# Layer 3 of a GNN stack: the keys split into two equal halves, and a tile's logits issued in two runs

## The chip, the cores and the metric

The kernel runs on one core of a Trainium2 chip. A core has a tensor engine (TensorE, PE in the profile, with its weight loads listed apart as PEld), VectorE (DVE), ScalarE (ACT), GpSimd (POOL) and SyncE (SP), each with an instruction queue of its own that is served in order, and DMA queues that move data between device memory and the on-chip memory. Matmuls write to PSUM, which has eight banks of 512 f32 values on each of 128 partitions. The metric is the device time of one execution, in microseconds (us).

## The reference

Four graph layers over 3327 nodes with 256 features, each a residual block `x = x + layer(relu(layernorm(x)))`. The change touches the last one, which runs two steps of attention with nucleus (top-p) sparsification beside a propagation by the row-normalized adjacency:

```python
def _top_p_attention(X, W1, W2, W3):
    q = X @ W1.T @ W2.T
    k = X @ W3.T
    logits = q @ k.T / TAU
    probs = jax.nn.softmax(logits, axis=-1)
    ...
    keep_sorted = cs - sp < TOP_P
    ...
    A = probs * mask
    return A / jnp.maximum(A.sum(-1, keepdims=True), 1e-12)
...
for n in range(STEPS):
    A = _top_p_attention(Xa, W1, W2, W3)
    Xf = R @ Xf
    Xa = A @ Xa
    Z = Z + Xf @ U1[n].T + Xa @ U2[n].T
h = X + Z
```

The queries and keys have 64 features. All of it is f32. So for each of 128 query rows a full row of 3327 logits is made, exponentiated, cut at the smallest set of entries that holds 0.9 of its sum, and multiplied with the 3327 x 256 values.

## The kernel before

**Tiles.** Nodes stand in T = 26 tiles of P = 128 (3328, one row more than there are nodes); H = 13 is half of them. Layers 0 to 2 take the first 950 us or so and are not touched, except that their last stage fills the first step's keys.

**Keys and queries.** A key has 64 features and PE 128 rows, so the keys lie in two halves of the partitions: `kT` has the first LOW = 12 tiles of keys on partitions 0 to 63 and the other HIGH = 14 on partitions 64 to 127 (`add_nodes`, L233; `new_keys`, L256). `add_nodes` computes key and query of one tile of nodes with two matmuls (L241), lets ACT copy the key into its half with a running sum for the mean (L249) and the query into qT (L253), and a DMA from ACT's queue copies the query to the other half too (L254). `centre` (L893) takes the mean off the keys on DVE, one instruction for each half.

**A tile's logits.** `logits_steps` (L904) is a generator. In each of the first three turns it makes one pair of PSUM banks from the pool `ps_row` (two buffers of two banks): one matmul of the low 64 partitions with 512 keys of the low half (L912), one of the high 64 partitions with 512 keys of the high half, into the two banks. ACT evicts both with one exponential of 1024 columns into the row e, and a sum into one column of `parts` (L935). The fourth turn makes the 255 keys that are left, of the high half alone (L921). POOL clears the last column of e beforehand (L931), in `scores`; the general path (`redone`) does the same at L1171.

**The search.** `search_steps` (L939) finds the threshold of each row. DVE sums `parts` (total, L951); ACT takes its logarithm and from that a first threshold (mean, lnv, c, t at L952 to L956); ACT runs two passes over e (L967, L969); DVE runs two more passes (L977, and L986 in four pieces with 26 MAX8 of 128 columns, L990), five rounds of the largest eight (v, L995 and L998), and at the end one pass that zeroes what is not kept (L1006).

**Attention times values.** `rows_times_steps` (L168) turns e by blocks of 128 on PE (L177, four blocks to a bank of `ps_tr`), ACT copies them out (eT, L180), and PE multiplies them with the values (L188), 26 matmuls of 256 columns. `Rows.begin` turns the first two groups of four blocks ahead of time, `Rows.finish` does the rest.

**Propagation.** `propagated_steps` (L1051) is the other product: 26 matmuls (f, L1062) with a tile's 26 blocks of the adjacency, loaded by SP as two slabs of 13 blocks (L1059, three buffers); POOL adds the identity to the block on the diagonal (L1061). It yields after each block, and a plan, a dictionary from block number to a list of functions, says what PE is given behind which block.

**The order.** PE's instructions are in the order in which they are recorded (`manual_schedule`); the other engines' orders are set by a scheduler. A period of the first step, for tile m: finish the attention of m (with the first two passes of the search of a later tile put behind its first groups), then propagate m + 3 with this plan: the four turns of the logits of tile m + 3 behind blocks 0, 2, 4 and 6 (`spread`, L1295), the attention's result turned behind block 3 (`turn`), its key and query made behind 10 (`node`), its values behind 14 (`values`), and the next tile's first two groups turned behind 22 (`rows.begin`). The second step has the four turns at the same blocks and `rows.begin` behind 22; `finish3` ends with a normalization on DVE and POOL (L1126 to L1138) and stores the output. At the start of either step a few tiles are prepared first: in step 0 tile 0's logits go behind blocks 9, 11, 13 and 15 of the second propagation and tile 1's behind 0, 2, 4 and 6 of the third; in step 1 tile 0's come alone, and tiles 1 and 2 are spread over one propagation each, with `PropagationOfFirstStep.turn` behind block 2 and `sums` (L1115) behind 10. At the end of step 0 (m from 20 on) there is no propagation in the period, and the turns come one behind the other.

Of the kernel before, what the change touches and what calls it, by code (L numbers as in the profile page):

```python
# [11 lines left out]
F32 = mybir.dt.float32  # L12
# [9 lines left out]
N = 3327  # L22
D = 256
DA = 64
P = 128
T = 26
NP = T * P
LAST = N - (T - 1) * P
NC = D // P
H = T // 2  # L30
# [1 line left out]
TOPK = 700  # L32
TOP_P = 0.9
EPS = 1e-5
LOW = 12
HIGH = T - LOW
Z90 = 1.2815516
PDF90 = 0.1754983
# [7 lines left out]
def kernel(  # L46
# [22 lines left out]
    nc = tc.nc  # L69
# [186 lines left out]
    def new_keys(name, pool):  # L256
        kT = pool.tile([P, HIGH * P], F32, tag="kT", name=f"kT_{name}")
        ksum = pool.tile([P, T], F32, tag="ksum", name=f"ksum_{name}")
        nc.gpsimd.memset(ksum, 0.0)
        return kT, ksum  # L260


# [576 lines left out]
    def layer_3_in(tag, big, ep, w3, sm3, h3, kT0, ksum0, left):  # L839
# [59 lines left out]
                    k = kT[r : r + DA, :n]  # L899
                    nc.vector.tensor_scalar(k, k, mean[r : r + DA, :], None, ALU.add)  # L900

        CHUNKS = (NP - 256) // 1024

        def logits_steps(kT, q, e, name, evict):  # L904


            main = e[:, : CHUNKS * 1024].rearrange("p (h c n) -> p h c n", h=2, n=512)
            for c in range(CHUNKS + 1):
                pl = ps_row.tile([P, 2, 512], F32, tag="row", name=f"pl_{name}_{c}")
                if c < CHUNKS:  # L910
                    for h in range(2):
                        nc.tensor.matmul(  # L912
                            pl[:, h, :], q[h * DA : (h + 1) * DA, :],
                            kT[h * DA : (h + 1) * DA, c * 512 : (c + 1) * 512],
                            start=True, stop=True,
                        )
                    evict(c, main[:, :, c, :], pl)
                    yield c
                else:
                    n = N - CHUNKS * 1024  # L920
                    nc.tensor.matmul(  # L921
                        pl[:, 0, :n], q[DA:, :], kT[DA:, c * 512 : c * 512 + n], start=True, stop=True
                    )
                    evict(c, e[:, CHUNKS * 1024 : N], pl[:, 0, :n])
                    yield c

        def scores(step, m, kT):

            name = f"{tag}{step}_{m}"
            e = ep.tile([P, NP], F32, tag="e", name=f"e_{name}")  # L930
            nc.gpsimd.memset(e[:, N:], 0.0)  # L931
            parts = sm3.tile([P, CHUNKS + 1], F32, tag="parts", name=f"parts_{name}")

            def evict(c, dst, src):
                nc.scalar.activation(dst, src, AF.Exp, accum_out=parts[:, c : c + 1])  # L935

            return e, parts, logits_steps(kT, qT[:, m * P : (m + 1) * P], e, name, evict)
# [230 lines left out]

        def redone(step, m, kT, name, evict):
            e = ep.tile([P, NP], F32, tag="e", name=f"e_{name}")  # L1170
            nc.gpsimd.memset(e[:, N:], 0.0)  # L1171
            run(logits_steps(kT, queries(step, m, name), e, name, evict))
            return e

# [91 lines left out]
        with tc.manual_schedule(engines=PE_ALONE):  # L1266

            st0, made, dens, props = new_state("0"), {}, {}, []

            def prepare(step, m, kT):  # L1270
                made[m] = scores(step, m, kT)
                return made[m][2]

            def find(step, m, st):
                return search_steps(step, m, *made[m][:2], st, dens)

            def passes(finder):


                if finder is None:  # L1280
                    return {}
                next(finder)

                def one_more():
                    with tc.issue_after(last_turned[-1].ins):
                        next(finder, None)

                return {0: [one_more], 2: [one_more], 3: [lambda: next(finder, None)]}

            def propagate_first(m, at):  # L1290
                acc = new_acc(f"f0_{m}")
                run(propagated_steps(acc, 0, m, h3), at)
                props.append(PropagationOfFirstStep(m, acc))

            def spread(steps, first=0, gap=2):  # L1295

                return {first + gap * i: [lambda: next(steps, None)] for i in range(CHUNKS + 1)}

            class Rows:


                def __init__(self, step, values):
                    self.step, self.values, self.begun = step, values, {}

                def begin(self, m):
                    if m < T:
                        name = f"a{self.step}_{m}"
                        accs = []

                        def acc():  # L1310
                            accs.append(new_acc(name))
                            return accs[0]

                        steps = rows_times_steps(acc, made.pop(m)[0], self.values, w3, name)
                        next(steps)
                        self.begun[m] = steps, accs

                def finish(self, m, at=None):
                    steps, accs = self.begun.pop(m)
                    run(steps, at)  # L1320
                    return accs[0]

            for i in range(EARLY):
                if i == 0:
                    left.pool = w3, "eT", 3
                    propagate_first(0, dict(zip((14, 20), ([what] for what in left.stages))))
                    mean0 = key_sum(kT0, ksum0, "0")
                elif i == 1:
                    steps = prepare(0, 0, kT0)
                    propagate_first(1, merged({3: [lambda: centre(kT0, mean0(), "0")]}, spread(steps, 9)))  # L1330
                    run(find(0, 0, st0))
                else:
                    first, second = prepare(0, i - 1, kT0), None
                    propagate_first(i, spread(first))
                    finder = find(0, i - 1, st0)
                    run(finder)
            run(prepare(0, EARLY - 1, kT0))
            finder = find(0, EARLY - 1, st0)
            rows = Rows(0, h3)
            rows.begin(0)  # L1340
            for m in range(T):
                plan = passes(finder)
                if props:
                    p = props.pop(0)
                    plan = merged(plan, {1: [p.turn], 5: [p.sums]})
                a = AttentionOfFirstStep(m, rows.finish(m, plan), dens.pop(m), f"{m}")
                after = {3: [a.turn], 10: [a.node], 14: [a.values], 22: [lambda: rows.begin(m + 1)]}
                steps = prepare(0, m + AHEAD, kT0) if m + AHEAD < T else iter(())
                if m + EARLY < T - LATE:
                    propagate_first(m + EARLY, merged(spread(steps), after))  # L1350
                else:
                    run(steps)
                    for k in sorted(after):
                        after[k][0]()
                finder = find(0, m + AHEAD, st0) if m + AHEAD < T else None
            flags0 = failed("0", st0)
            propagate_first(T - LATE, {})
# [11 lines left out]
        with tc.manual_schedule(engines=PE_ALONE):  # L1369
            centre(kT1, key_sum(kT1, ksum1, "1")(), "1")  # L1370
            st1 = new_state("1")
            run(prepare(1, 0, kT1))
            run(find(1, 0, st1))
            for i in range(1, LATE):
                plan = spread(prepare(1, i, kT1))
                p = props.pop(0)
                propagate_first(T - LATE + i, merged(plan, {2: [p.turn], 10: [p.sums]}))
                finder = find(1, i, st1)
                if i + 1 < LATE:
                    run(finder)  # L1380
            p = props.pop(0)
            p.turn()
            p.sums()

            def propagate_second(m, at):
                acc = new_acc(f"f1_{m}")
                run(propagated_steps(acc, 1, m, fs), at)
                return acc

            rows = Rows(1, vs)  # L1390
            rows.begin(0)
            for m in range(T):
                acc = rows.finish(m, passes(finder))
                y = attention_of_second_step(m, acc, dens.pop(m), f"{m}")
                plan = spread(prepare(1, m + AHEAD, kT1)) if m + AHEAD < T else {}
                plan = merged(plan, {22: [lambda: rows.begin(m + 1)]})
                finish3(m, y, propagate_second(m, plan), f"{m}")
                finder = find(1, m + AHEAD, st1) if m + AHEAD < T else None
            flags1 = failed("1", st1)
# [77 lines left out]
```

## Time and profile before

| what | us |
|---|---|
| three runs, median | 2720.22 (2718.76 to 2723.25) |
| the profiled execution | 2722.73 |
| its span, first to last instruction | 2720.9 |
| first propagation of layer 3 begins on PE | 956 |
| step 0 of layer 3, periods with propagation and logits | 1022.85 to 1722.86 |
| its last six tiles and step 1's start | 1722.86 to 1930.63 |
| step 1, periods with logits | 1930.63 to 2627.83 |

The profile's page lists busy time by engine, the span in 40 slices, the DMA queues, the chain that ended last, and the costliest groups of instructions. In a group or a timeline row, `f<-fsa,slab3a 128*128 128x256 f32` is output, inputs, weights (rows x columns) and output (partitions x columns); `x8` counts instructions, and a bracket gives the idle time of the engine ahead of the row and what ended it. The granted TensorE clock, in tenths, and the busy share of PE in the same 40 slices (68 us each):

```profile
PE   7999999999999979999999999987999999999997
...
PEclk9999999999999999999999999998999999999998
```

PE is nearly always busy; the slices with less are the kernel's start and end, the start of layer 3 (slice 15 from the left) and the end of step 0 with the start of step 1 (slices 27 and 28); the clock is lower in slice 28 and at the end. The exponential that evicts a pair of banks, and then the two groups that make a tile's logits, in step 1 and in step 0, from the listing of PE's groups:

```profile
L935 ACT ACTIVATE e_a<-pl_a 128x1024 f32<-128x1024 f32 x208 | 179.4, 863 | 183.4 <-PE pl_a L912 150.4
```

```profile
L912 PE MATMUL pl_a<-kT_1a,qT 64*128 64x512 f32 x312 | 92.0, 665 | 6.6 <-ACT e_a L935 5.0 <-DMA slab3a<-in_adj_t_dram 1.5
L912 PE MATMUL pl_a<-kT_0a,qT 64*128 64x512 f32 x312 | 87.0, 638 | 2.3 <-ACT e_a L935 2.3
L921 PE MATMUL pl_a<-kT_1a,qT 64*128 64x255 f32 x52 | 18.5, 437 | 0.0
L921 PE MATMUL pl_a<-kT_0a,qT 64*128 64x255 f32 x52 | 18.1, 427 | 0.0
```

Behind the bar stand the busy time of the group in us, the mean of one in ns, and the idle time of the engine just ahead of it with what ended it. The durations of matmuls that run side by side or overlap in the pipeline add up to more than they take; what they cost is better read from the starts of the rows behind them in a timeline.

### The profile page before, as it was taken

Reading aid. Unit: us, or ns where it says so; the run is one execution under the profiler, and the core shown is the slowest. Engines: PE = TensorE matmul, PEld = TensorE weight load, DVE = VectorE, ACT = ScalarE, POOL = GpSimd, SP = SyncE. Lnnn points to the kernel's source line nnn. Section 1 sums busy time; section 2 is a strip of 40 time slices with the busy share of each in tenths; the row PEclk is TensorE's granted clock in tenths of the full one; section 3 lists DMA queues with packets and bytes.
Section 4 is the critical chain, followed back from the end, with each engine's and each line's share of the span. In section 5 each row is a group of like instructions: output and inputs, shape, how many; then the busy total and the mean of one; then the engine's idle time right before and its main releaser. Section 6 shows DMA issues by size and latency. Waiting matters only on the chain. (4 is left out here: it accounts for less than half of the span.)

```text
span 2720.9 us, 42472 instructions
## 1 busy us (share of the span) xinstructions
PE 2629.9 (97%) x15875; PEld 2203.2 (81%) x15875; DVE 2034.0 (75%) x5488; ACT 1046.3 (38%) x1877; POOL 215.3 (8%) x384
## 2 busy tenths in 40 slices
PE   7999999999999979999999999987999999999997
PEld 6999999999999957777777777665777777777786
DVE  6676788888877758666666666892888878887882
ACT  2111034332011145445444445554444454445441
POOL 2000010000000010000000000000111111111111
PEclk9999999999999999999999999998999999999998
DMA  7555555555666530111111111001211221122111
GB/s 219 150 156 163 167 155 168 174 173 172 190 192 201 151 113 33 59 60 60 59 60 60 59 58 59 24 10 50 83 65 63 76 76 66 63 71 79 68 63 51
DMA packets 141356, 273.41 MB, mean 100 GB/s; under 512 B 15427, under 2 KB 67904, under 8 KB 141120
## 3 DMA queue, kind: packets, MB, share of 16 engines
q1 hardware_dynamic: 115648, 252.49, 29.2%
q10 hardware_dynamic: 25472, 17.92, 2.2%
q8 instruction: 131, 2.15, 0.3%
q14 instruction: 105, 0.86, 0.1%
HBM read 248.20 MB, written 20.45 MB: 99 GB/s over the span
## 5 line engine op out<-in xcount | busy, mean ns | idle before, releaser
L1062 PE MATMUL f<-h3a,slab3a 128*128 128x256 f32 x1352 | 338.1, 388 | 0.2 <-POOL ok L1026 0.2
L188 PE MATMUL a<-h3a,eT_a 128*128 128x256 f32 x1352 | 325.0, 382 | 8.9 <-ACT eT_a L180 5.7
L180 ACT COPY eT_a<-pt_a 128x512 f32<-128x512 f32 (+1 forms) x364 | 195.6, 553 | 350.7 <-PE pt_a L177 347.1
L1062 PEld LDWEIGHTS f<-h3a,slab3a 128*128 128x128 f32 x1352 | 244.5, 190 | 99.3 <-issue 72.3
L1062 PE MATMUL f<-fsa,slab3a 128*128 128x256 f32 x1352 | 324.8, 385 | 0.0
L188 PE MATMUL a<-vs,eT_a 128*128 128x256 f32 x1352 | 322.5, 383 | 0.4 <-ACT eT_a L180 0.2
L1062 PEld LDWEIGHTS f<-fsa,slab3a 128*128 128x128 f32 x1352 | 246.2, 189 | 90.0 <-issue 59.9
L990 DVE MAX8 cand_a<-w 128x8 f32<-128x128 f32 x1352 | 282.9, 279 | 5.9
L188 PEld LDWEIGHTS a<-h3a,eT_a 128*128 128x128 f32 x1352 | 245.6, 190 | 45.0 <-ACT eT_a L180 15.9
L188 PEld LDWEIGHTS a<-vs,eT_a 128*128 128x128 f32 x1352 | 246.3, 190 | 37.3 <-ACT eT_a L180 6.3
L518 PE MATMUL acc_a<-tsa,s_a 128*128 128x128 f32 (+1 forms) x2028 | 268.4, 275 | 0.7 <-DVE tsa L330 0.7
L518 PE MATMUL acc_a<-tsa,a_a 128*128 128x128 f32 x2028 | 250.3, 275 | 1.8 <-DVE tsa L333 1.8
L518 PE MATMUL acc_a<-rhs,a_a 128*128 128x128 f32 (+1 forms) x2028 | 250.4, 276 | 0.0
L935 ACT ACTIVATE e_a<-pl_a 128x1024 f32<-128x1024 f32 x208 | 179.4, 863 | 183.4 <-PE pl_a L912 150.4
L518 PEld LDWEIGHTS acc_a<-tsa,s_a 128*128 128x128 f32 x2028 | 247.4, 192 | 1.2 <-DVE tsa L330 1.0
L518 PEld LDWEIGHTS acc_a<-tsa,a_a 128*128 128x128 f32 x2028 | 239.1, 192 | 3.0 <-DVE tsa L333 2.2
L518 PEld LDWEIGHTS acc_a<-rhs,a_a 128*128 128x128 f32 x2028 | 238.4, 192 | 1.9 <-ACT rhs L410 0.4
L971 DVE TENSOR_SCALAR u_a<-sign_a 128x1 f32<-128x1 f32 x52 | 8.0, 154 | 295.7 <-ACT junk_a L969 295.7
L986 DVE SCALAR_TENSOR_TENSOR w<-e_a,t_a 128x896 f32<-128x896 f32 x208 | 224.8, 1081 | 4.2
L177 PE MATMUL pt_a<-ident,e_a 128*128 128x128 f32 x1352 | 200.5, 274 | 15.3 <-DVE e_a L1006 13.1
L177 PEld LDWEIGHTS pt_a<-ident,e_a 128*128 128x128 f32 x1352 | 166.0, 141 | 56.5 <-DVE e_a L1006 13.5
L977 DVE SCALAR_TENSOR_TENSOR w<-e_a,t_a 128x3328 uint8<-128x3328 f32 x52 | 191.6, 3684 | 3.6
(203 smaller groups left out, 3515.3 us busy)
## 6 DMA issues: line engine op xcount, KB each, us to landing
slab3a<-in_adj_t_dram SPq DMA_DIRECT2D x104, 832.0 KB, 5.9
a_a<-in_adj_t_dram SPq DMA_DIRECT2D x312, 256.0 KB, 3.3
a_a<-in_adj_t_dram SPq DMA_DIRECT2D x156, 320.0 KB, 3.4
x_dram<-x_a ACTq DMA_DIRECT2D x39, 256.0 KB, 2.8
x_a<-x_dram SPq DMA_DIRECT2D x26, 256.0 KB, 3.1
hT_dram<-xT_a ACTq DMA_DIRECT2D x26, 128.0 KB, 3.7
hT<-hT_dram SPq DMA_DIRECT2D x26, 128.0 KB, 2.0
z_dram<-z SPq DMA_DIRECT2D x26, 128.0 KB, 1.7
```

The source lines that it names most:

```text
L177: nc.tensor.transpose(pt[:, j, :], e[:, k * P : (k + 1) * P], ident)
L180: last_turned.append(nc.scalar.copy(eT[:, : len(blocks), :], pt[:, : len(blocks), :]))
L188: nc.tensor.matmul(acc[:, :width], ready[g][:, j, :], rhs[:, k, :], start=(k == 0), stop=(k == T - 1))
L518: nc.tensor.matmul(self.acc[:, g, at : at + wide], quads[n][:, k - CUTS[c][0], :], t, start=(k == 0 and n in (1, 4)), stop=(k == H - 1 and ...
L935: nc.scalar.activation(dst, src, AF.Exp, accum_out=parts[:, c : c + 1])
L971: nc.vector.tensor_scalar(u, sign, 0.5, NP / 2 - AIM, ALU.mult, ALU.add)
L977: nc.vector.scalar_tensor_tensor(junk, e, t, e, ALU.is_lt, ALU.mult, accum_out=got)
L986: nc.vector.scalar_tensor_tensor(w[:, : (b - a) * P], eg, t, eg, ALU.is_lt, ALU.mult, accum_out=below[:, g : g + 1])
L990: nc.vector.max(cand[:, 8 * k : 8 * k + 8], w[:, (k - a) * P : (k - a + 1) * P])
L1062: nc.tensor.matmul(acc[:, :D], slab[g][:, j, :], xf[:, k, :], start=(n == 0), stop=(n == T - 1))
```

## The change

The keys are split evenly, 13 tiles on either half of the partitions (LOW = H). A tile's logits are then four pairs of banks, three of 512 columns on either half and one of 128, and the missing 3328th key is a column of zeros in `kT`, whose exponential is 1; a further column of `parts` holds -1 so that the total is right. POOL clears the last column of e behind the last eviction instead of ahead of the logits. The generator yields twice instead of four times, each time with two pairs of banks: behind blocks 0 and 12 in step 0 (9 and 19 for tile 0, 0 and 10 for tile 1), behind 0 and 10 in step 1. `node` goes from block 10 to 9, `values` from 14 to 18, and the first two groups of the next tile are turned behind block 20 instead of 22, in both steps.

```diff
-LOW = 12
+LOW = H
...
         nc.gpsimd.memset(ksum, 0.0)
+        nc.gpsimd.memset(kT[DA:, HIGH * P - 1 :], 0.0)
         return kT, ksum
...
-        CHUNKS = (NP - 256) // 1024
+        CHUNKS = [(c, min(c + 512, LOW * P)) for c in range(0, LOW * P, 512)]
 
         def logits_steps(kT, q, e, name, evict):
-            main = e[:, : CHUNKS * 1024].rearrange("p (h c n) -> p h c n", h=2, n=512)
-            for c in range(CHUNKS + 1):
+            halves_of_e = e.rearrange("p (h n) -> p h n", h=2)
+            for c, (a, b) in enumerate(CHUNKS):
                 pl = ps_row.tile([P, 2, 512], F32, tag="row", name=f"pl_{name}_{c}")
-                if c < CHUNKS:
-                    for h in range(2):
-                        nc.tensor.matmul(
-                            pl[:, h, :], q[h * DA : (h + 1) * DA, :],
-                            kT[h * DA : (h + 1) * DA, c * 512 : (c + 1) * 512],
-                            start=True, stop=True,
-                        )
-                    evict(c, main[:, :, c, :], pl)
-                    yield c
-                else:
-                    n = N - CHUNKS * 1024
+                for h in range(2):
                     nc.tensor.matmul(
-                        pl[:, 0, :n], q[DA:, :], kT[DA:, c * 512 : c * 512 + n], start=True, stop=True
+                        pl[:, h, : b - a], q[h * DA : (h + 1) * DA, :], kT[h * DA : (h + 1) * DA, a:b],
+                        start=True, stop=True,
                     )
-                    evict(c, e[:, CHUNKS * 1024 : N], pl[:, 0, :n])
+                evict(c, halves_of_e[:, :, a:b], pl[:, :, : b - a])
+                if c == len(CHUNKS) - 1:
+                    nc.gpsimd.memset(e[:, N:], 0.0)
+                if c % 2:
                     yield c
 
         def scores(step, m, kT):
...
-            nc.gpsimd.memset(e[:, N:], 0.0)
-            parts = sm3.tile([P, CHUNKS + 1], F32, tag="parts", name=f"parts_{name}")
+            parts = sm3.tile([P, len(CHUNKS) + 1], F32, tag="parts", name=f"parts_{name}")
+            nc.gpsimd.memset(parts[:, len(CHUNKS) :], -1.0)
...
-            def spread(steps, first=0, gap=2):
-                return {first + gap * i: [lambda: next(steps, None)] for i in range(CHUNKS + 1)}
+            def spread(steps, first=0, second=10):
+                return {k: [lambda: next(steps, None)] for k in (first, second)}
...
-                    propagate_first(1, merged({3: [lambda: centre(kT0, mean0(), "0")]}, spread(steps, 9)))
+                    propagate_first(1, merged({3: [lambda: centre(kT0, mean0(), "0")]}, spread(steps, 9, 19)))
...
-                after = {3: [a.turn], 10: [a.node], 14: [a.values], 22: [lambda: rows.begin(m + 1)]}
+                after = {3: [a.turn], 9: [a.node], 18: [a.values], 20: [lambda: rows.begin(m + 1)]}
...
-                    propagate_first(m + EARLY, merged(spread(steps), after))
+                    propagate_first(m + EARLY, merged(spread(steps, 0, 12), after))
...
-                plan = merged(plan, {22: [lambda: rows.begin(m + 1)]})
+                plan = merged(plan, {20: [lambda: rows.begin(m + 1)]})
```

In `redone`, too, the clear of e's last column ahead of the logits goes away.

## The prediction

> **What bounds the kernel now.** I read the page's busy table first, then PE's timeline over one period of layer 3's second step, then DVE's and ACT's over the same period, then the places where PE stands still. The page:
>
> ```profile
> PE 2629.9 (97%) x15875; PEld 2203.2 (81%) x15875; DVE 2034.0 (75%) x5488; ACT 1046.3 (38%) x1877; POOL 215.3 (8%) x384
> ```
>
> PE's timeline (start, us, engine, line, out<-in, form, count; PE runs each f32 matmul as two passes, which count as two instructions):
>
> ```profile
> 2264.13 1.89 PE L188 MATMUL a<-vs,eT_a 128*128 128x256 f32 x8
> ...
> 2277.74 0.59 PE L1062 MATMUL f<-fsa,slab3a 128*128 128x256 f32 x2
> 2278.26 1.13 PE L912 MATMUL pl_a<-kT_1a,qT 64*128 64x512 f32 x4
> 2279.32 1.13 PE L1062 MATMUL f<-fsa,slab3a 128*128 128x256 f32 x4
> 2280.39 1.13 PE L912 MATMUL pl_a<-kT_1a,qT 64*128 64x512 f32 x4
> 2281.44 1.13 PE L1062 MATMUL f<-fsa,slab3a 128*128 128x256 f32 x4
> 2282.51 1.13 PE L912 MATMUL pl_a<-kT_1a,qT 64*128 64x512 f32 x4
> 2283.57 1.13 PE L1062 MATMUL f<-fsa,slab3a 128*128 128x256 f32 x4
> 2284.63 0.69 PE L921 MATMUL pl_a<-kT_1a,qT 64*128 64x255 f32 x2
> 2285.25 7.18 PE L1062 MATMUL f<-fsa,slab3a 128*128 128x256 f32 x32
> 2292.26 1.04 PE L177 MATMUL pt_a<-ident,e_a 128*128 128x128 f32 x8
> 2293.14 1.46 PE L1062 MATMUL f<-fsa,slab3a 128*128 128x256 f32 x6
> 2294.44 1.89 PE L188 MATMUL a<-vs,eT_a 128*128 128x256 f32 x8
> ```
>
> No row ends with a bracket of idle time: PE is never kept waiting, and the next tile's L188 starts 30.31 us after this one's. Finish starts in PE's timeline at 1930.63 and 2627.83 enclose 23 such periods of step 1 (697.2 us), 1022.85 and 1722.86 enclose 20 of step 0 (700.0, 34.95 each but for the first). There the length of PE's own work sets the time. ACT and DVE in the same period:
>
> ```profile
> 2288.08 0.20 ACT L952 ACTIVATE mean_a<-total_a 128x1 f32<-128x1 f32 x1 [2.25 <-DVE total_a L951]
> 2289.16 0.20 ACT L956 ACTIVATE t_a<-t_a 128x1 f32<-128x1 f32 x1 [0.23 <-DVE t_a L955]
> 2292.90 1.07 ACT L180 COPY eT_a<-pt_a 128x512 f32<-128x512 f32 x2 [3.53 <-PE pt_a L177]
> ```
>
> DVE does wait, 3.19 us a period ahead of L971 for ACT's second pass and 0.98 for POOL ahead of L1135, so a period shorter by 1 us still fits its work.
>
> **Part 1, logits.** Between 2277.74 and 2292.26 lie 14.52 us with 46 instructions of f. One of those takes 0.216 (eight of L188: 2264.13 to 2265.85 is 1.72), so f needs 9.94 and a tile's logits cost 4.58. Their price splits by another place, the end of step 0, where the four groups of one tile follow each other with nothing between:
>
> ```profile
> 1738.82 1.99 PE L912 MATMUL pl_a<-kT_0a,qT 64*128 64x512 f32 x8
> 1741.17 1.13 PE L912 MATMUL pl_a<-kT_0a,qT 64*128 64x512 f32 x4 [0.36 <-ACT e_a L935]
> ```
>
> Eight instructions take 1.99 and four take 1.13: a second pair of banks right behind the first costs 0.86, so its two halves stream side by side and nothing is paid again. A lone pair plus the two f blocks behind it takes 2.12 (2278.26 to 2280.39); less four f (0.86) and the pair's own 0.86 this leaves 0.40 for going from 128-row to 64-row weights and back. The 255-wide rest costs two passes at 0.21 and the same 0.40. Four trips: 4 x 0.40 + 3 x 0.86 + 0.42 = 4.60, against 4.58 found.
>
> After: two trips, three full pairs, one pair of 128 columns, a quarter of 0.86: 2 x 0.40 + 3 x 0.86 + 0.22 = 3.60. Gain 1.00 per tile: 0.80 from the trips, 0.20 from the columns. No row shows a 64-row matmul of 128 columns. Its bounds are 0.22 (L177's 128-column transposes, each with weights of its own, run at 0.109: 2292.26 to 2293.14 for eight) and 0.42 (no gain over L921). I take 0.22, since L177 has the same width; the other end takes back 0.20 x 43 = 9.
> On this the sum: 20 tiles in step 0 and 23 in step 1 at 1.00: **-43**.
>
> **Part 2, who else is moved.** The built order of the changed kernel shows the queues. Moving the first turned blocks from 22 to 20 costs PE nothing: the same eight transposes. It matters for ACT, whose queue holds the chain mean, lnv, c, t in front of the two copies of eT, and mean waits for DVE's total. In step 1 total now stands behind the last of the 26 MAX8, about 15.6 us after L971 (L991 was at 2290.28, L971 at 2274.55); then total, mean, lnv, c (1 us by ACT's rows) and t, which now stands behind DVE's second round of v, make the first eT ready 28.4 us after the finish starts. PE needs it at 30.31 - 1.00 = 29.3: 0.9 to spare. In step 0 total is behind the fifth v, and vs is copied ahead of eT: by the rows from 1469.57 to 1474.80, ready at 32.8, needed at 33.95. Node goes from block 10 to 9 and values from 14 to 18; node's two ACT copies (1470.68 to 1471.44 now, behind the chain; in the new order ahead of the third exp) leave the bank 1.5 us before the fourth pair wants it. DVE's z of values comes some 1.2 us later into the next period; its bank is next asked for 15 us after that, and the z store holds up two slab loads behind it on SP (issued 1.1 us into a period now) whose blocks come over 20 us later. All of this costs nothing; each us by which node's copies or the loads came too late would be PE's.
>
> The clearing of e's last column moves from ahead of the logits to behind the fourth exp, on POOL (0.10 us, as L931 now). Behind the clear in POOL's queue stand the new clear of parts (0.1, its tile is four old) and the diagonal add of the next slab; waiting for the clear are the first pass (L967) and so everything behind that on ACT. The fourth exp ends some 26 us into a period and the pass comes 2.8 us into the next: over 6 us of cover, and every us beyond it would be PE's. Total reads five columns for four (0.14 now); both key tiles are centred over 1664 and 1663 columns for 1536 and 1791, the same sum; kT's clear is two small POOL rows in setup.
>
> **Part 3, the two openings.** Step 0: tile 0 gets its groups at blocks 9 and 19 instead of 9, 11, 13, 15. By the rates above the fourth pair ends at 983.3 (now 982.6), but two exps of 1.02 and 0.38 stand behind each other, so the search starts 1.6 later; PE waits for that search anyway (13.14 us idle at 1021.06, released by L1006): **+1.6**. Tile 1's two trips are hidden by the same wait.
>
> Step 1, tile 1:
>
> ```profile
> 1885.45 1.03 PE L1062 MATMUL f<-h3a,slab3a 128*128 128x256 f32 x4
> 1891.44 2.08 PE L912 MATMUL pl_a<-kT_1a,qT 64*128 64x512 f32 x4 [4.96 <-ACT e_a L935]
> 1893.45 2.07 PE L1062 MATMUL f<-h3a,slab3a 128*128 128x256 f32 x4
> ```
>
> PE stands 4.96 us because ACT runs tile 0's passes before it evicts, and the rows behind are at half speed (2.08 for 1.13) until 1900. After, six more f blocks run before the third pair: PE stops at 1888.6 and still goes on at 1891.4, so the stall shrinks to 2.8; then sums waits 0.9 for a bank. If half speed follows all the same, 2.7 us are won; if not, 7.1. The rows show half speed after 4.96 and none after 1.60 (1748.67); 2.8 lies between, and I take **-5**. Tile 2 gains its 1.0 and loses 0.85 to sums: nothing.
> The Trainium skill ("TensorE: Matmul & The Clock Gate", What's actually happening) says that PE falls to half clock after an idle window of about 3.4 us. By that a 2.8 us stall leaves PE at full speed and the sum would be 2 us lower; the 4.96 row agrees with it, and nothing so far shows 2.8.
>
> The three tiles of step 0 with all groups together (m 20 to 22) are set by DVE's and ACT's chain (25.87 us a period, eT late by 1.60): nothing.
>
> **Sum.** -43 + 1.6 - 5 = -46.4. The profiled execution took 2722.7 (span 2720.9 and 1.8 around it) and would take 2676.3; the median of the runs, 2720.2, lies 2.5 below it, so I write **2674**.
>
> **Rivals.**
> (a) *Joining pays less*: every pair pays its way in again, only columns are won: 43 x 0.20 = 9, less 3: about 2708. Against: 1.99 for eight. A pair takes 0.86 and its exp 1.02 + 0.19, so a third pair in a row stalls (the 0.36 above); here runs are of two.
> (b) *The copies come late*: t or total slips and the search chain (28.4 and 32.8 us) sets the period. Half of part 1 is lost if the chain is 1.4 us longer in step 1 and 1.65 in step 0: 20 less: about 2695.
> (c) *Slower*: the clear of e's column is served behind the next slab's diagonal add, which now lands 6.2 us into a period of step 0 (1449.41, after 29.52 us of waiting for its DMA). The first pass, due at 2.8, and the eT copies behind it would come at 6.6, PE would stall 3.8: step 0 gets 20 x 2.8 = 56 longer, step 1 keeps -23, the openings -3: 2750. Decides from 1 us of lateness. For it: POOL serves in order, and at step 1's start a slab add does stand ahead. Against: in the steady stretch the built order has e's clear in front of that add.
>
> **Chances.** Forecast 0.80, (a) 0.04, (b) 0.11, (c) 0.05. The likeliest case runs from 2668 (opening won in full, the first opening free, trips dearer by 0.05) to 2685 (128 columns at 0.42, the opening at 2.7); reaching into (b) gives 2666 to 2692 for 8 in 10. A run of this kernel tells some 0.2% (5 us) from no change. Faster 0.94, same 0.02, slower 0.04.
>
> **What would show it.** Finish starts 33.95 and 29.31 apart; L912 x8 of 1.99 and the second run 1.6 long; no idle ahead of L188; idle ahead of the third pair in step 1's opening near 2.8, full speed behind it or not. Wrong if L188 waits for eT, if a 128-column pair takes over 0.4, or if POOL's clear waits for a DMA.

## The result, and the profile after

The changed kernel takes 2676.39 us (median of four runs, 2674.28 to 2678.22) against 2720.59 for the kernel before beside it: a ratio of 0.9837, 95% interval 0.9819 to 0.9854. The forecast was 2674, faster, in a range of 2666 to 2692. The profiled execution took 2678.22, with a span of 2676.3.

Lines have moved: in the changed kernel f is L1058, all logits L912, the exp L931, e's clear L918, total L947, the chain mean to t L948 to L952, DVE's last pass L1002, the slab's diagonal add L1057 and values L1082. The page's busy table after:

```profile
PE 2581.7 (96%) x15979; PEld 2219.4 (83%) x15979; DVE 2038.3 (76%) x5488; ACT 1035.3 (39%) x1877; POOL 219.1 (8%) x438
```

PE is busy 48.2 us less than before; DVE and ACT run as many instructions as they did. PE's timeline over the step 1 period that was shown of before:

```profile
2274.32 0.59 PE L1058 MATMUL f<-fsa,slab3a 128*128 128x256 f32 x2
2274.84 1.99 PE L912 MATMUL pl_a<-kT_1a,qT 64*128 64x512 f32 x8
2276.76 4.58 PE L1058 MATMUL f<-fsa,slab3a 128*128 128x256 f32 x20
2281.28 1.35 PE L912 MATMUL pl_a<-kT_1a,qT 64*128 64x512 f32 x8
2282.56 4.58 PE L1058 MATMUL f<-fsa,slab3a 128*128 128x256 f32 x20
2286.98 1.03 PE L177 MATMUL pt_a<-ident,e_a 128*128 128x128 f32 x8
2287.85 2.32 PE L1058 MATMUL f<-fsa,slab3a 128*128 128x256 f32 x10
2290.01 1.89 PE L188 MATMUL a<-vs,eT_a 128*128 128x256 f32 x8
```

Four groups have become two. The second lasts 1.28 from its start to f's next, with the 128-column pair in it (the group's row names the form of its first pair). No row carries a bracket of idle time. Finish starts at 1908.86 and 2583.13 enclose 23 periods of step 1: 674.27 us, 29.31 each. Those at 1025.83 and 1706.36 enclose 20 of step 0: 680.53, 33.96 each but for the first (35.28, whose first rows run at half speed behind the opening's last wait).

ACT's chain and the first two copies of eT in that period (ACT's timeline):

```profile
2287.17 0.20 ACT L948 ACTIVATE mean_a<-total_a 128x1 f32<-128x1 f32 x1 [3.24 <-DVE total_a L947]
2288.41 0.20 ACT L952 ACTIVATE t_a<-t_a 128x1 f32<-128x1 f32 x1 [0.37 <-DVE t_a L951]
2288.52 1.05 ACT L180 COPY eT_a<-pt_a 128x512 f32<-128x512 f32 x2
```

The first copy is done about 2289.05, 28.35 us behind the finish start of 2260.70, and PE asks for it at 29.31.

The spans differ by 44.6 us. Read from the starts in the two PE timelines:

| part of the span | before to after, us |
|---|---|
| up to step 0's first logits (not touched) | 975.67 to 977.12: +1.45 |
| from there to step 0's first finish | 47.18 to 48.71: +1.53 |
| 20 periods of step 0 | 700.01 to 680.53: -19.48 |
| from there to step 1's first logits | 151.51 to 151.05: -0.46 |
| step 1's opening, to the first finish | 56.26 to 51.45: -4.81 |
| 23 periods of step 1 | 697.20 to 674.27: -22.93 |
| the rest | +0.1 |

From step 0's first logits to the end layer 3 takes 1699.2 us for 1745.2, so the change is worth 46.0 in one execution. The time ahead of that point wanders by itself: it was 972.98 to 979.36 over the profiles of this study, and no edit touches it. So openings are compared below by their own lengths.

### The profile page after: what moved, and what is told of

It is laid out like the page before. It is cut to its first block, busy times and chain, and to the rows that moved or that the text cites. A ratio compares the mean times of both kernels' runs of the same rounds, so it can differ in the third digit from the quotient of the medians.

```text
span 2676.3 us, 42731 instructions
## 1 busy us (share of the span) xinstructions
PE 2581.7 (96%) x15979; PEld 2219.4 (83%) x15979; DVE 2038.3 (76%) x5488; ACT 1035.3 (39%) x1877; POOL 219.1 (8%) x438
## 5 line engine op out<-in xcount | busy, mean ns | idle before, releaser
L1058 PE MATMUL f<-h3a,slab3a 128*128 128x256 f32 x1352 | 323.6, 383 | 0.2 <-issue 0.2
L1058 PE MATMUL f<-fsa,slab3a 128*128 128x256 f32 x1352 | 312.5, 382 | 0.0
L1058 PEld LDWEIGHTS f<-h3a,slab3a 128*128 128x128 f32 x1352 | 247.7, 190 | 60.4 <-issue 28.1
L1058 PEld LDWEIGHTS f<-fsa,slab3a 128*128 128x128 f32 x1352 | 249.8, 189 | 52.8 <-issue 16.7
L931 ACT ACTIVATE e_a<-pl_a 128x1024 f32<-128x1024 f32 x208 | 177.9, 860 | 205.8 <-PE pl_a L912 205.7
L973 DVE SCALAR_TENSOR_TENSOR w<-e_a,t_a 128x3328 uint8<-128x3328 f32 x52 | 191.6, 3684 | 3.6
```

The costliest lines, as they stand in the source:

```text
L973: nc.vector.scalar_tensor_tensor(junk, e, t, e, ALU.is_lt, ALU.mult, accum_out=got)
L1058: nc.tensor.matmul(acc[:, :D], slab[g][:, j, :], xf[:, k, :], start=(n == 0), stop=(n == T - 1))
```

## The experiments

The kernel before ran beside every batch, at medians of 2720.6 to 2722.9.

### The two halves of the gain, each alone

*Joining alone.* The keys lie 12 and 14 tiles to a half again; the two runs stay.

```diff
-LOW = H
+LOW = 12
 ...
-        CHUNKS = [(c, min(c + 512, LOW * P)) for c in range(0, LOW * P, 512)]
+        CHUNKS = 3
 ...
+                    nc.tensor.matmul(
+                        pl[:, 0, :n], q[DA:, :], kT[DA:, c * 512 : c * 512 + n], start=True, stop=True
+                    )
 ...
                 if c % 2:
                     yield c
```

> The joining alone: two runs a tile as in the changed kernel, but the keys lie 12 and 14 tiles to a half as before, so a run is two pairs, and then one pair and the lone 255-column rest (no extra column of sums and no clear of it). Theory (trips 0.40 each, columns 0.20 a tile): step 0 period 34.95 - 0.80 = 34.15, step 1 period 30.31 - 0.80 = 29.51, openings as in the changed kernel, so 43 x 0.20 = 9 above it: 2685. Rival, each pair pays its way in again and only the columns were worth something: periods back near 34.95 and 30.31, about 2717.

Measured: 2686.47 (2684.39 to 2689.23), ratio 0.987 [0.9854, 0.9887]; periods of 34.16 and 29.52. PE's timeline has the second run as

```profile
2260.51 1.13 PE L912 MATMUL pl_a<-kT_1a,qT 64*128 64x512 f32 x4
2261.48 0.59 PE L920 MATMUL pl_a<-kT_1a,qT 64*128 64x255 f32 x2
```

where the rest occupies 0.52 up to f's next start (2262.00). The rival (nothing from joining) would have left the periods near 34.95 and 30.31.

*The even split alone.* Every pair by itself again, two blocks apart.

```diff
-                if c % 2:
-                    yield c
+                yield c
 ...
-                return {k: [lambda: next(steps, None)] for k in (first, second)}
+                return {k: [lambda: next(steps, None)] for k in (first, first + 2, second, second + 2)}
```

> The even split alone: keys of 13 tiles on either half, three full pairs and one of 128 columns as in the changed kernel, but each pair goes by itself, two f blocks apart (four trips a tile). Theory: periods 34.95 - 0.20 = 34.75 and 30.31 - 0.20 = 30.11, tile 0 of step 0's opening 1 us later than in the changed kernel: 2676.4 + 43 x 0.80 + 1 = 2712. Rival, the short pair costs as much as the 255-column rest did (0.42): 2720, nothing won by the columns. Rival, a short pair by itself costs a trip of its own only in part: 2700 or below.

Measured: 2709.95 (2707.75 to 2713.56), ratio 0.9963 [0.9949, 0.9977]; periods 34.70 and 30.11. PE's timeline:

```profile
2302.52 1.13 PE L912 MATMUL pl_a<-kT_1a,qT 64*128 64x512 f32 x4
2303.58 1.13 PE L1057 MATMUL f<-fsa,slab3a 128*128 128x256 f32 x4
2304.64 0.49 PE L912 MATMUL pl_a<-kT_1a,qT 64*128 64x128 f32 x4
2305.06 3.72 PE L1057 MATMUL f<-fsa,slab3a 128*128 128x256 f32 x16
```

A full pair alone takes 1.06 up to the next start, the short one 0.42: the difference, 0.64, is three quarters of 0.86. So both halves of the forecast gain stand alone at their size: in step 1 the joining is worth 30.31 - 29.52 = 0.79 a tile, the columns 30.31 - 30.11 = 0.20. In step 0, by 34.95, 34.16 and 34.70, they are 0.79 and 0.25.

### One run in place of two

```diff
+            def at_once(steps):
+                return {0: [lambda: next(steps, None), lambda: next(steps, None)]}
 ...
-                    propagate_first(m + EARLY, merged(spread(steps, 0, 12), after))
+                    propagate_first(m + EARLY, merged(at_once(steps), after))
 ...
-                plan = spread(prepare(1, m + AHEAD, kT1)) if m + AHEAD < T else {}
+                plan = at_once(prepare(1, m + AHEAD, kT1)) if m + AHEAD < T else {}
```

> In the steady periods of both steps all four pairs of a tile go behind block 0 in one run (one trip less a tile; openings as in the changed kernel). Theory: the trip saves 0.40, but the third pair waits for the first exp's bank and the short one for the second's; where a tile's pairs stand in one run already, at the end of step 0, the third starts 0.44 late and the four take about 3.8 us for 3.2 streamed, so 0.2 a tile more than two runs: periods 34.15 and 29.5, 43 x 0.2 = 9 slower, 2685. Rival, ACT is earlier in the steady periods and the waits vanish: 0.40 a tile faster, 2659.

Measured: 2694.17 (2690.23 to 2695.42), ratio 0.9903 [0.9886, 0.9919]; periods 34.33 (34.45 in the last ones of step 0) and 29.69: slower, as forecast, but by 0.37 to 0.38 a tile and not 0.2. PE's timeline:

```profile
2282.99 1.99 PE L912 MATMUL pl_a<-kT_1a,qT 64*128 64x512 f32 x8
2285.33 1.50 PE L912 MATMUL pl_a<-kT_1a,qT 64*128 64x512 f32 x8 [0.36 <-ACT e_a L931]
2286.76 8.90 PE L1058 MATMUL f<-fsa,slab3a 128*128 128x256 f32 x40
```

The miss is one of bookkeeping. The run takes 3.77. What streams in it is 3 x 0.86 + 0.22 = 2.80, and of a trip's 0.40 only 0.20 lies in the run's own rows (1.92 for the first run of the changed kernel, 1.72 streamed). The rest lies in the neighbours: f's two instructions ahead take 0.53 for 0.43, and the 20 behind the first run 4.52 for 4.32, which holds one run's exit and the next one's entry. So the waits for the banks are 3.77 - 2.80 - 0.20 = 0.77, dearer than the trip saved by 0.37. The expectation had counted the whole trip into the run.

### The other moves taken back

```diff
-                after = {3: [a.turn], 9: [a.node], 18: [a.values], 20: [lambda: rows.begin(m + 1)]}
+                after = {3: [a.turn], 10: [a.node], 14: [a.values], 22: [lambda: rows.begin(m + 1)]}
 ...
-                plan = merged(plan, {20: [lambda: rows.begin(m + 1)]})
+                plan = merged(plan, {22: [lambda: rows.begin(m + 1)]})
```

> The changed kernel with the moves of the other steps taken back: first turned blocks behind block 22, node behind 10, values behind 14. Theory: the moves cost and won nothing; the eT copies wait for t and not for PE, so step 1 stays at 29.31; in step 0 the bank of values may be asked for up to 0.2 us early, so 33.96 to 34.15: 2676 to 2680. Rival, the earlier turn is what let the copies keep up: PE waits for eT ahead of L188 in step 1, 0.3 us or more a period, 2683 or above.

Measured: 2680.59 (2678.42 to 2685.26), ratio 0.9849 [0.9832, 0.9865]. Step 1 stays at 29.31 to the hundredth, so turning at 20 or 22 is one there, and the rival falls. Step 0 has 34.15 and, in its last seven periods, 34.28 for 33.96. The groups of instructions name the place; PEld is PE's weight load, the last column its idle time. In this kernel, and then in the changed one:

```profile
L1082 PEld LDWEIGHTS u<-u2s,xT_a 128*128 128x128 f32 x104 | 17.7, 190 | 20.0 <-issue 12.4 <-ACT e_a L931 7.5
```

```profile
L1082 PEld LDWEIGHTS u<-u2s,xT_a 128*128 128x128 f32 x104 | 19.2, 189 | 13.6 <-issue 12.5
```

With values two blocks behind the second run, its bank (from the pool of the logits) is still held by an exp: 7.5 us of waiting, 20 times. The periods of step 0 are 0.19 to 0.32 longer. All three moves were taken back at once; the wait names values, and a share of node or of the turned blocks in step 0 is not told apart. The move of values to 18 wins nothing over before; it keeps the joined runs from costing that.

### How late e's clear may come

To price the slower rival (c), the clear of e's column was written many times over, so that POOL ends it late.

```diff
-                    nc.gpsimd.memset(e[:, N:], 0.0)
+                    for _ in range(400):
+                        nc.gpsimd.memset(e[:, N:], 0.0)
```

> The cover of e's clear: 400 clears of the same column in place of one, one behind the other on POOL (the page's setup rows show four in 0.19, so at 0.03 each 12 to 13 us, with a wait between them up to 0.10 each and 40 us). The single clear ran at 2283.99 and the first pass of the next period at 2292.86 in step 1, 1461.81 and 1471.47 in step 0: 8.8 and 9.6 us of cover. Theory: what the clears take beyond the cover, some 3 to 4 us or more, is added to each period in full: at 12.8 us, 23 x 4.0 + 20 x 3.2 = 156 longer, 2832, and PE waits for eT ahead of L188 in the middle of a finish. Rival: ACT and DVE have the slack to take the late pass (DVE waits 2 to 3 us a period): under 1 us a period, below 2720.

Measured: 4017.27 against 2832 expected. The size was off: a clear takes 0.08 (829 in 62.57 us) to 0.16 in such a row and not 0.03, so the 400 last some 57 us in step 0 and set the whole period. The second try had 90:

> The cover of e's clear once more, with 90 clears in place of 400, since a clear took 0.10 to 0.155 us there (89 in 8.86, 86 in 13.36) and not 0.03: 9 to 14 us against covers of 8.8 (step 1) and 9.6 (step 0). Theory, lateness beyond the cover is added to each period in full and costs nothing below it: at 0.13 a clear 11.7 us, so 2.9 x 23 + 2.1 x 20 = 109 longer, 2785 (2676 if they take 9, 2880 if 14), PE waiting for eT in the middle of a finish. Rival, the cover is shorter than the two starts say, or longer because ACT and DVE have slack: the periods grow by over 1 us more or less than the clears' end beyond the due time of the first pass.

Measured: 3057.32, ratio 1.1233, far above the 2785 expected and the 2880 for clears of 14 us. POOL's timeline, then ACT's, then PE's, in step 0 (finish start 1581.15):

```profile
1574.27 0.57 POOL L919 MEMSET e_a<- 128x1 f32 x4 [24.76 <-ACT e_a L932]
1577.09 0.10 POOL L929 MEMSET parts_a<- 128x1 f32 x1 [2.25 <-DVE total_a L948]
1577.13 13.42 POOL L919 MEMSET e_a<- 128x1 f32 x86
```

```profile
1590.58 3.07 ACT L964 ACTIVATE junk_a<-e_a,t_a 128x3328 uint8<-128x3328 f32 x1 [6.49 <-POOL e_a L919]
```

```profile
1594.27 1.11 PE L177 MATMUL pt_a<-ident,e_a 128*128 128x128 f32 x4 [6.68 <-ACT eT_a L180]
```

The clears end at 1590.55, 16.3 us after the first began: among them stands the clear of `parts`, which waits 2.25 for DVE, and that was not in the expectation. The pass is due 2.84 behind the finish start (1471.47 after 1468.63 in the changed kernel), at 1583.99: 6.6 late, and PE stands 6.7. This period is 42.95, one of the longest, 9.0 more than in the changed kernel; the mean is 7.3 more in step 0 (827.1 us for 680.5) and 7.2 in step 1 (838.8 for 674.3). What goes beyond PE's wait, 2.3 here, comes with the rows behind it at half speed (1.11 for 0.60), which was not in the sum either. So the cover is what the two starts say, 1583.99 - 1574.27 = 9.7 us, and lateness beyond it is paid in full and more. The rival's sign, a growth over 1 us off the lateness, did come, but by the half speed: the wait itself is the lateness. In the changed kernel POOL's timeline has

```profile
1461.81 0.10 POOL L918 MEMSET e_a<- 128x1 f32 x1 [19.62 <-ACT e_a L931]
...
1475.63 0.45 POOL L1057 TENSOR_TENSOR slab3a<-slab3a,ident 128x128 f32<-128x128 f32 x1 [10.36 <-DMA slab3a<-in_adj_t_dram]
```

with the clear in front of the add that waits for its DMA, so rival (c) has no occasion.

### The openings

*Step 0.* Tile 0's second run behind block 11:

```diff
-                    propagate_first(1, merged({3: ...}, spread(steps, 9, 19)))
+                    propagate_first(1, merged({3: ...}, spread(steps, 9, 11)))
```

> The changed kernel with tile 0's second run of step 0's opening behind block 11 and not 19. Theory (the +1.5 of this opening is the later second run, and PE's wait there for the search of tile 0 passes every us on): the second run starts near 980.0 for 983.55, its exps follow the first run's at once, total of tile 0 is read near 982.4 for 986.24, and the first finish starts 3 to 4 us earlier: 2672.5 to 2673.5, against 2676.4. Rival: DVE, which has tiles 1 and 2 to serve in between, sets the end of that wait: under 1 us, 2676.

Measured: 2666.90 (2666.00 to 2667.72), ratio 0.9803 [0.9788, 0.9818], more than was expected. The opening is 40.03 long for 48.71. Total comes 3.45 us sooner behind the first logits (5.67 for 9.12), as reckoned; the other 5.2 lie between total and the end of tile 0's last pass (37.7 in the changed kernel, 32.5 here), where DVE's order is another. Its timeline in the changed kernel, then in this one:

```profile
1012.05 3.68 DVE L973 SCALAR_TENSOR_TENSOR w<-e_a,t_a 128x3328 uint8<-128x3328 f32 x1
...
1020.30 3.67 DVE L1002 SCALAR_TENSOR_TENSOR e_a<-e_a,all_least 128x3328 f32<-128x3328 f32 x1
```

```profile
1007.47 3.69 DVE L1002 SCALAR_TENSOR_TENSOR e_a<-e_a,all_least 128x3328 f32<-128x3328 f32 x1
...
1011.96 3.68 DVE L973 SCALAR_TENSOR_TENSOR w<-e_a,t_a 128x3328 uint8<-128x3328 f32 x1
```

L973 is tile 1's pass, L1002 tile 0's last one, for which PE waits. DVE now serves tile 0 to the end first, and PE's wait there falls from 10.91 to 0.95, while its wait ahead of tile 2's second run grows from 4.98 to 7.47.

*Step 1.* Tiles 1 and 2 with later second runs and sums:

```diff
-                plan = spread(prepare(1, i, kT1))
+                plan = spread(prepare(1, i, kT1), 0, 18)
 ...
-                propagate_first(T - LATE + i, merged(plan, {2: [p.turn], 10: [p.sums]}))
+                propagate_first(T - LATE + i, merged(plan, {2: [p.turn], 22: [p.sums]}))
```

> The changed kernel with the second runs of step 1's opening (tiles 1 and 2) behind block 18 and not 10, and the sums beside them behind 22 and not 10. Theory: by then ACT has done tile 0's passes, so PE does not stand for 2.74 and 0.75 us, and the half speed from 1875 to 1881 goes too: tile 2's first run at about 1881 for 1887.55. The finish can't start before DVE ends tile 0's last pass (1901.86), where PE stood at 1907.58 so far, so of 6.5 us at most 5.7 count: 2670.7. Rival, half speed is not due to the standing: 3.5 us, 2673. Rival, the later exps of tile 1 push the search back and PE waits for that: 2676 or above.

Measured: 2675.12 (2674.56 to 2676.26). The opening is 51.01 for 51.45: nothing, for runs that leave this opening as it is have 50.46 to 52.15. The two old waits are gone, and PE's timeline has a new one, with half speed behind it:

```profile
1882.82 2.08 PE L912 MATMUL pl_a<-kT_1a,qT 64*128 64x512 f32 x4 [3.78 <-ACT fsa L1113]
```

PE now comes to tile 2's pairs while ACT runs tile 1's passes in front of the sums' eviction. Both openings together:

> Both openings moved as in the two runs before this one. Theory: the gains add, 3.5 and 5.7, so 2667. Rival: the first is swallowed by what follows in step 0 or the second by DVE: 2671 or above.

Measured: 2668.11 (2665.37 to 2669.94): the first gain is kept, the second is not there. Two more tries, both with step 0's opening moved too, put tile 2's runs behind 14 and 25 and its sums behind 24, and then its turn at 13 for 2 (not in this diff):

```diff
-                plan = spread(prepare(1, i, kT1))
+                plan = spread(prepare(1, i, kT1), *((0, 18), (14, 25))[i - 1])
 ...
-                propagate_first(T - LATE + i, merged(plan, {2: [p.turn], 10: [p.sums]}))
+                propagate_first(T - LATE + i, merged(plan, {2: [p.turn], (22, 24)[i - 1]: [p.sums]}))
```

> The changed kernel with step 0's opening as before (second run of tile 0 behind block 11) and step 1's opening mended where the last try failed: tile 1's second run behind 18 and its sums behind 22; tile 2's first run behind 14 and its second behind 25, with the sums behind 24. Theory (there PE came to tile 2's second pair while ACT still ran tile 1's passes in front of the sums' eviction, stood 3.78 and fell to half speed): now the pair comes after that eviction, nothing is waited for, and the first finish of step 1 starts when DVE ends tile 0's last pass, 5 us earlier: 2667 - 5 = 2662. Rival, DVE's order is changed and tile 0's last pass moves back: 2667 or above.

Measured: 2670.12 (2667.91 to 2672.24), opening 51.03. PE's timeline:

```profile
1876.21 0.69 PE L136 MATMUL pt_f<-ident,xf 128*128 128x128 f32 x2 [4.39 <-ACT xf L1099]
```

> The last try at the openings with one more move: in tile 2's propagation of step 1's opening the turn stands behind block 13 and not 2 (in the last run PE came to that turn at 1872 and stood there until 1876.7, since ACT copies xf between tile 1's two passes). Theory: PE now has 13 blocks to work on while ACT runs the first pass, stands nowhere over 1 us and keeps full speed; from the first logits to the first finish 51.03 falls to about 45.4, where DVE's last pass of tile 0 (ended 44.1 us behind the first logits) sets the start: 2670 - 5.6 = 2664.5, and 1684.5 from step 0's first logits to the end of the span (1690.0). Rival: another wait of PE on ACT takes its place (the sums' bank, the second turned pair), under 2 us won: 2668 or above and 1688 or more.

Measured: 2669.99 (2668.62 to 2673.11). Up to the finish PE stands nowhere over 1.5 us, and then, in PE's and ACT's timelines:

```profile
1900.83 3.78 PE L188 MATMUL a<-vs,eT_a 128*128 128x256 f32 x8 [4.33 <-ACT eT_a L180]
```

```profile
1900.10 0.20 ACT L948 ACTIVATE mean_a<-total_a 128x1 f32<-128x1 f32 x1 [5.74 <-DVE total_a L947]
1900.21 1.05 ACT L180 COPY eT_a<-pt_a 128x512 f32<-128x512 f32 x2
```

The copies of eT stand behind tile 2's mean, and mean waits for a total that DVE reaches late: rival (b)'s mechanism, found in an opening. The opening is 49.60, and the first period is 32.18 for 29.42, its first rows at half speed, so nothing is won. Each wait taken away let the next one through, and whether this opening has anything to give stays open. The lowest median here is that of step 0's opening alone moved (2666.90); the runs with both moved overlap it (2665.37 to 2669.94).

## Why the prediction was right, point by point

*Part 1* forecast 1.00 a tile. The 23 periods of step 1 gave 22.93, the 20 of step 0 19.48 (the first gave only 0.33: 35.28 for 35.61, both with half speed in them), 42.4 for 43. Its split stands too: 0.79 and 0.20 by the two runs of one half each, for 0.80 and 0.20. The value chosen for the 128-column pair, 0.22, is the one found, by the 0.64 between it and a full pair; rival (a), that joining pays nothing, falls.

*Part 2* forecast nothing. The margins came out as worked: first eT at 28.35 for 28.4 in step 1, 32.5 for 32.8 in step 0 (copies from 1466.68, finish from 1434.67). e's clear had 9.7 and 8.8 us (2283.99 to 2292.86) where the text said over 6. Rival (b) had its mechanism right, as the last try at the openings shows, but in the steady periods there is room. What the text did not see is that the late place of values is needed: with it at 14 again (and the other moves taken back), step 0 loses 0.19 to 0.32 a period.

*Rival (c)* was priced at a stall of 3.8 a period, the lateness in full, less the 1.0 that part 1 wins: 2.8. The clears show the lateness in full, as priced, and half speed on top, which the price left out.

*Part 3* forecast +1.6 for step 0's opening; 1.53 was found, and in the way it said. DVE read tile 0's total 7.59 us behind the first logits before and 9.12 after, and from there to the end of the pass for which PE waits it took 37.7 in both. DVE's timeline before, then after:

```profile
983.26 0.16 DVE L951 TENSOR_REDUCE total_a<-parts_a 128x1 f32<-128x4 f32 x1 [7.79 <-ACT e_a L935]
```

```profile
986.24 0.16 DVE L947 TENSOR_REDUCE total_a<-parts_a 128x1 f32<-128x5 f32 x1 [9.32 <-ACT e_a L931]
```

What it did not see is that DVE's order left 5.2 to win there.

For step 1's first tile it forecast -5; tile 2's first logits came 4.92 sooner, 0.1 of it given back up to the finish. The waits were 2.74 and 0.75 for 2.8 and 0.9. PE's timeline:

```profile
1873.55 1.59 PE L912 MATMUL pl_a<-kT_1a,qT 64*128 64x512 f32 x8 [2.74 <-ACT e_a L931]
1875.89 2.07 PE L1111 MATMUL u<-u1s,hT 128*128 128x256 f32 x4 [0.75 <-ACT e_a L931]
```

The prediction left open whether half speed follows. In a table of stretches (busy time of each engine, then PEclk, the granted clock, third from the end):

```profile
1873.50:1874.50 1.00, 0.95 (x4) 0.30 (x4) 0.89 (x1) 1.00 (x2) 0.00 (x0) 1.00 0.00 0
1875.80:1877.70 1.90, 1.81 (x4) 1.51 (x5) 1.90 (x7) 0.66 (x5) 0.20 (x2) 0.50 0.00 0
1879.40:1881.00 1.60, 1.60 (x5) 1.27 (x4) 1.56 (x8) 1.20 (x3) 0.00 (x0) 0.50 0.09 29
1881.40:1883.40 2.00, 2.00 (x10) 1.69 (x10) 1.97 (x10) 2.00 (x2) 0.00 (x0) 0.94 0.03 8
```

The pair behind the 2.74 began at 1.00. In stretches of 0.1 us the clock falls to 0.50 at 1874.8, ahead of the further 0.75, and is back at 1881.7. So half speed did follow, for 6.8 us, where the kernel before had 10.2 (1891.0 to 1901.2).

Other runs stand at the same place for the same time, and there the clock falls at other moments. With only step 0's opening moved, in PE's timeline and the table of stretches:

```profile
1861.83 2.50 PE L912 MATMUL pl_a<-kT_1a,qT 64*128 64x512 f32 x8 [2.72 <-ACT e_a L931]
```

```profile
1861.83:1862.83 1.00, 1.00 (x2) 0.50 (x4) 0.94 (x1) 0.95 (x2) 0.00 (x0) 0.50 0.00 0
```

Here the clock fell 0.2 us before the stall was over. It also fell before the end in the runs with joining alone and with the moves taken back (2.73 each); with one run in place of two, behind a stall of 2.68, it fell only within the further one (0.85) and was back 3.4 us later. In the changed kernel and the three of these runs that leave this opening's code alone it is 50.46 to 52.15 long, so the change wins 4.1 to 5.8 there. The -5 was chosen between two cases, 2.7 with half speed as long as before and 7.1 with none; neither came, but a half speed that was shorter. The shrinking of the stall was worked out, the value behind it was partly luck.

The rule of the Trainium skill ("TensorE: Matmul & The Clock Gate", What's actually happening) was used as if one stall were held against 3.4 us. By that reading the opening would have won 7. Four profiles show the clock falling on a stall of 2.72 to 2.74 us alone, so the measurement decides against that reading. The same section of the Trainium skill says that the window is free-running. That fits the changing moment of the fall, and so do the lengths of half speed, 3.4, 6.8 and 10.2 us; how much idle time in a window it takes is not shown, for none of these stalls fills 3.4 us.

*The sum* was -46.4, and layer 3 became 46.0 shorter in the profiled executions. The medians differ by 44.2, and the median of the changed kernel, 2676.39, lies 2.4 above the forecast. In the profiled pair 1.45 went to a later start of layer 3. The four runs of the changed kernel spread over 3.9 us, and the time ahead of layer 3 wandered by 6.4 over the profiles, so what the 2.4 are is not shown. Taking off 2.5, by which one profiled execution stood above its median, added an accuracy that the runs do not have.

## What to carry to other kernels

Price a switch between two tilings by rows with and without it, and count the neighbours' rows: of 0.40 us there and back only half lay in the group itself. Joining groups pays as long as the eviction keeps up: two pairs in a run fit two bank sets here, four waited 0.77 to save 0.40. Where one engine waits for another's search in an opening, look first at whose work the other serves before it: that order was worth 5 us in step 0, and moving PE's waits about in step 1 nothing.

## What the runs showed of the hardware

A one-column clear on POOL took 0.156 us in a row of 86 that write the same column (13.42 us), and 0.10 in one of 89 (8.86), while four of different tiles in the setup took 0.19 together.

Stalls of 3.78, 4.33, 4.39 and 6.68 us on PE were each followed by rows at about half speed (2.08 for 1.13, 3.78 for 1.89, 0.69 for 0.38, 1.11 for 0.60). So were the five of 2.68 to 2.74 in step 1's opening. Stalls of 0.62, 1.60, 2.25 and 2.38 were not. In that opening the clock fell 2.35 to 4.83 us after PE had stopped, and it stayed at 0.50 for 3.4 us (one run in place of two), 6.8 (the changed kernel and others) or 10.2 (the kernel before).
